# The two ends of a causal attention kernel: x ahead of the weights, filler on the identity, the last sums on TensorE, the third half inverted through DRAM

## The chip, the cores and the metric

The kernel runs on one core of one Trainium2 chip. The metric is the device time of one execution in microseconds (us). Before the change it is the median of three runs. The profile is one execution taken by the hardware profiler; its times count from the first instruction, and its span is a little shorter than the time of the run.

## The reference

One layer over x of shape (32, 256, 32, 32), all in float32. x is normalised over groups of 8 channels, projected to queries, keys and values by 1x1 convolutions, and attention with 8 heads of 32 dimensions runs over the 1024 positions of each image. A position sees only positions before it; the first one sees none. The result is added to x.

```python
q = jnp.einsum('oc,bcs->bos', q_w, xf) + q_b[None, :, None]
kv = jnp.einsum('oc,bcs->bos', kv_w, xf) + kv_b[None, :, None]
k, v = (kv[:, :EMBED_C], kv[:, EMBED_C:])
...
mask = jnp.tril(jnp.ones((S, S), dtype=x.dtype), -int(MASK_CENTER))
scores = jnp.einsum('bhqd,bhkd->bhqk', q, k) / jnp.sqrt(jnp.asarray(dk, x.dtype))
scores = jnp.where(mask == 0, jnp.asarray(-10000.0, x.dtype), scores)
attn = jax.nn.softmax(scores, axis=-1)
attn = jnp.where(mask == 0, jnp.asarray(0.0, x.dtype), attn)
out = jnp.einsum('bhqk,bhkd->bhqd', attn, v)
...
x = x + _L0_conv_ref(_gn(x), L0_conv_q_w, L0_conv_q_b, L0_conv_kv_w, L0_conv_kv_b)
```

## The kernel before

**Tiling.** Channels lie on the 128 partitions in two groups (`NG = 2`, four heads each); the 1024 positions are cut into two halves of 512 (`NH = 2`). Group and half together give four results per image, numbered n = 0 to 3, each a tile of 128 x 512. Scores are computed transposed, keys on partitions, without a shift by the maximum: `scores` (L303) makes them on TensorE, ScalarE takes exponentials into tiles `e` (four heads x 512) and `eh` (four heads x 256), GpSimd cuts the diagonal (`mask`, L285). `values` (L341) multiplies by v into `acc`, one visit later, and VectorE adds the exponentials up in the first `e` tile of each result, called `total` (L358). The denominator is the sum of `total` over the partitions, a product with a matrix of ones (`sum_keys`, L388, result `pd`).

**Order.** An image is N = 12 visits. The list `visits` says which pieces of scores a visit makes, `products` which pieces are multiplied after it. Everything else of an image hangs on a visit number: `at` holds calls made after the scores of a visit, `after` calls made after its values. The order of TensorE, ScalarE, VectorE and GpSimd is the order in which the program writes the calls (`tc.manual_schedule`). Each engine runs its queue in that order, so an instruction that waits holds back all that stand behind it. SyncE issues loads and stores, also in one order; ScalarE issues the loads of the weights and biases.

**Start.** x of images 0 and 1 is loaded on SyncE in halves by channel group (`load`, L113). ScalarE issues the three weights, the query bias, the key bias and the value bias (`load_weights`, L134). TensorE turns each weight by transposing products (`turn_weights`). VectorE takes the statistics (`norm_channels`), TensorE averages them over a group of channels (`norm_mean`, `norm_variance`), VectorE forms the variance (`norm_deviation`, tile `dev`), GpSimd the power of -1/2, VectorE the normalised x (`norm_apply`, tile `xn`). `keep_busy` (L151) makes products that nobody reads. The query bias is multiplied by the scale of the scores on VectorE at L566, behind `norm_apply`. Then the first projections (`pp`) run.

**Denominators.** For most images the totals are folded by DMA and inverted in a compact form: sums to DRAM, back as 128 rows of 64 (`gather`, tile `rows`), a check that they are in range and a reciprocal on VectorE (`check_sums`, `invert`), the inverses to DRAM, and from there broadcast to 32 partitions per head (tile `rb`). `finish` (L459) multiplies, adds the bias and x, and stores.

**End.** In the last image (b = 31) results 0 and 1 go that way, and GpSimd and ScalarE finish them (`finish_aside`). Results 2 and 3 are inverted in place: `check_here` and `invert_here` work on 128 x 512 tiles, the sum of the heads standing on all 32 partitions of each. The denominator of result 3 is put together on TensorE by `sum_pieces` (L395): first `total`, which VectorE has added up as far as visit N-2, and then the pieces of the last two visits, which aren't added on VectorE (`summed` is false in the last visit of scores and behind it). `end_last` (L492) checks and inverts result 3 in two halves of 256 columns; it also forms `outside`, the number that says whether any sum was out of range (then the whole is computed again in another way, which doesn't happen here).

```python
when(first + N, lambda b=b: check_here(2, in_range[:, ROW : ROW + 1]))
when(first + N, lambda b=b: invert_here(b, 2, slice(0, HALF)))
when(first + N, lambda b=b: finish(b, 2))
for n in every[:2]:
    when(first + N, lambda b=b, n=n: finish_aside(b, n), after)
```

Of the kernel before, what the change touches and what calls it, by code (L numbers as in the profile page):

```python
# [9 lines left out]
F32 = mybir.dt.float32  # L10
# [7 lines left out]
P = 128  # L18
HD = 32
CPG = 8  # L20
HALF = 512
# [10 lines left out]
def tile_norm_attention_residual(  # L32
# [64 lines left out]
        compare_op=ALU.is_ge, fill=0.0, base=CPG - 1, channel_multiplier=-1,  # L97
    )
    avg = avg.rearrange("p a b -> p (a b)")
    in_range = const.tile([P, ROW + 1], F32, name="in_range")  # L100
    nc.gpsimd.memset(in_range, 1.0)
    eps = const.tile([P, 1], F32, name="eps")
    nc.gpsimd.memset(eps, 1e-5)
# [5 lines left out]
    def unshifted():  # L109
# [1 line left out]
        bank_free = tc.alloc_semaphore("bank_free")  # L111
        xpool = tc.alloc_tile_pool(name="xpool", bufs=4)

        def load(b):
            live["x", b] = xpool.tile([P, NG, S], F32, tag="x", name=f"x_{b}")
            for g in range(NG):
                nc.sync.dma_start(out=live["x", b][:, g, :], in_=x_in[b, :, g, :])

        for b in range(min(2, B)):
            load(b)  # L120
        work = tc.alloc_tile_pool(name="work", bufs=2)
        qkpool = tc.alloc_tile_pool(name="qkpool", bufs=3)
        epool = tc.alloc_tile_pool(name="epool", bufs=3)
# [7 lines left out]
        def misc(name):  # L131
            return ps_m.tile([P, HALF], F32, tag="misc", name=name)
# [17 lines left out]

        def keep_busy(n):  # L151

            pt = ps_s.tile([P, 2, HALF], F32, tag="sT", name=f"busy_{n}")
            for _ in range(n):
                nc.tensor.matmul(pt[:, 0, :C], lhsT=ident, rhs=live["wn", 0][:, 0, :], start=True, stop=True)  # L155

        def spare(name):

# [233 lines left out]
                    start=start, stop=stop, skip_group_check=True,  # L392
                )

        def sum_pieces(b, pieces, start, stop):  # L395

            if start:
                live["pd", b] = misc(f"pd_{b}")
                sum_keys(live["pd", b], live["sum", b, NG - 1, NH - 1], slice(0, HALF), slice(0, HALF), True, False)
            for pc in pieces:  # L400
                e = live.pop(("e", b, pc))
                for kb, cols, of in pc[4]:
                    sum_keys(live["pd", b], e, cols, of, False, stop and pc is pieces[-1])

        def sums(b, g, hf):

            n = NH * g + hf
            total = live.pop(("sum", b, g, hf))
            if (b, n) == (B - 1, 3):
                pd = live["pd", b]  # L410
            else:
                pd = misc(f"pd_{b}_{n}")
                sum_keys(pd, total, slice(0, HALF), slice(0, HALF))
            den = small.tile([P, HALF], F32, tag="den", name=f"den_{b}_{n}")
            if b == B - 1 and n >= 2:

                most = small.tile([P, 1], F32, tag="most", name=f"most_{n}")
                nc.scalar.activation(den, pd, AF.Identity, accum_out=most)
                live["most", n], live["den", n] = most, pd if n == 3 else den
                return  # L420
            nc.scalar.copy(den, pd)
            if n == 0:
                live["sums", b] = dram.tile([4, 4, HALF], F32, tag="sums", name=f"sums_{b}")
            nc.sync.dma_start(out=live["sums", b][n], in_=den[::HD, :])
# [41 lines left out]
                nc.vector.tensor_copy(rb[:, 0:1], xt[:, g, 0:1])  # L466
            nc.sync.dma_start(out=x_out[b, :, g, cols], in_=rb)

        def check_here(n, ok):

            least = small.tile([P, 1], F32, tag="least", name=f"least_{n}")
            junk = small.tile([P, HALF], F32, tag="den", name=f"junk_{n}")
            nc.vector.tensor_scalar(junk, live["den", n], SUM_MIN, 1.0, ALU.is_ge, ALU.min, accum_out=least)
            nc.vector.scalar_tensor_tensor(ok, live["most", n], SUM_MAX, least, ALU.is_le, ALU.mult)

        def invert_here(b, n, within):
            rb = live["rb", b, n] if within.start else inverses(b, n)
            nc.vector.reciprocal(rb[:, within], live["den", n][:, within])  # L478

        def finish_aside(b, n):  # L480

            g, hf = divmod(n, NH)
            cols = slice(hf * HALF, (hf + 1) * HALF)
            num, rb, xt = live["num", b, n], live["rb", b, n], live["x", b]
            nc.gpsimd.tensor_tensor(rb, num, rb, ALU.mult)
            nc.gpsimd.tensor_tensor(rb, rb, xt[:, g, cols], ALU.add)
            nc.scalar.activation(rb, rb, AF.Identity, bias=v_bias_col[:, g : g + 1])
            if hf == 0:
                nc.scalar.copy(rb[:, 0:1], xt[:, g, 0:1])
            nc.sync.dma_start(out=x_out[b, :, g, cols], in_=rb)  # L490

        def end_last(b):  # L492


            worst = const.tile([P, 1], F32, name="worst")
            ok = const.tile([P, 1], F32, name="ok")
            nc.vector.tensor_reduce(worst, in_range, AX.X, ALU.min)
            check_here(3, ok)
            both = [slice(c * HALFBANK, (c + 1) * HALFBANK) for c in range(2)]
            invert_here(b, 3, both[0])  # L500
            pc = ps_o.tile([P, HALF], F32, tag="acc", name="pc")
            nc.tensor.matmul(pc[0:1, 0:1], lhsT=worst, rhs=ok, start=True, stop=True)
            outside = const.tile([1, 1], I32, name="outside")
            nc.vector.tensor_scalar(outside, pc[0:1, 0:1], -1.0, float(P), ALU.mult, ALU.add)
            finish(b, 3, both[0])
            invert_here(b, 3, both[1])
            finish(b, 3, both[1])
            return outside

# [39 lines left out]
        every = range(4)  # L549

        with tc.manual_schedule(engines={ENG.PE, ENG.Activation, ENG.DVE, ENG.Pool}):
            load_weights()
            turn_weights(0)
            for g in range(NG):
                norm_channels(0, g)
            keep_busy(2)
            norm_mean(0)
            turn_weights(1)
            norm_deviation(0)
            norm_variance(0)  # L560
            norm_rstd(0)
            turn_weights(2)
            keep_busy(4)
            for hf in range(NH):
                norm_apply(0, slice(hf * HALF, (hf + 1) * HALF))
            nc.vector.tensor_scalar_mul(qk_bias[:, 0, :], qk_bias[:, 0, :], SCALE)  # L566
            units = projections(0)
            for n, f in zip((None, None, 0, 0, 0, 0) + PROJECT[6:], units):
                if n is None:
# [5 lines left out]
            for b in range(B):  # L575
# [6 lines left out]
                    prepare(b, [first + n for n in PREPARE])  # L582
                for n in every:
                    v = first + (N if last and n == 3 else SUMS[n])
                    if last and n == 3:
                        for i in (N - 1, N):
                            when(first + i, lambda b=b, i=i: sum_pieces(b, products[i - 1], i == N - 1, i == N), after)
                    if late:
                        when(v, lambda b=b, n=n: sums(b, *divmod(n, NH)), after)
                    else:  # L590
                        when(v, lambda b=b, n=n: fold(b, n, 2 * HD), after)
                        when(v + 2, lambda b=b, n=n: fold(b, n, HD), after)
                        when(v + 4, lambda b=b, n=n: stack(b, n))
                if not last:
                    if not late:
                        when(first + N + 6, lambda b=b: sum_folded(b), after)
                    v = first + N + (2 if late else 8)
                    when(v, lambda b=b: gather(b, every))
                    when(v + 2, lambda b=b: check_sums(b, every))
                    when(v + 2, lambda b=b: invert(b, every))  # L600
                    for n in every:
                        when(first + FINISH[late][n], lambda b=b, n=n: finish(b, n), after)
                else:
                    when(first + N - 4, lambda b=b: gather(b, every[:2]))
                    when(first + N - 3, lambda b=b: check_sums(b, every[:2]))
                    when(first + N - 3, lambda b=b: invert(b, every[:2]))
                    when(first + N, lambda b=b: check_here(2, in_range[:, ROW : ROW + 1]))
                    when(first + N, lambda b=b: invert_here(b, 2, slice(0, HALF)))
                    when(first + N, lambda b=b: finish(b, 2))
                    for n in every[:2]:  # L610
                        when(first + N, lambda b=b, n=n: finish_aside(b, n), after)
            for i in range(B * N + 1):
                if i < B * N:

                    between = at.pop(i, ()) if i % N == 6 else ()
                    scores(i // N, *visits[i % N], between)
                for f in at.pop(i, ()):
                    f()
                if i:
                    for pc in products[(i - 1) % N]:  # L620
                        values((i - 1) // N, pc, i < B * N - 1)
                for f in after.pop(i, ()):
                    f()
            assert not at and not after
# [158 lines left out]
```

## Time and profile before

| | us |
|---|---|
| median of three runs | 1878.86 (1873.87, 1878.86, 1880.27) |
| the profiled run, and the span of its profile | 1876.05, 1874.0 |
| TensorE busy | 1850.8 |
| VectorE busy | 1573.4 |
| ScalarE busy | 1413.7 |
| GpSimd busy | 765.5 |
| first projection begins | 14.57 |
| last VectorE operation begins | 1869.20 |

Busy is the time in which an engine had an instruction under way. In the timeline each row has its start, its duration, the engine (PE is TensorE, PEld its loads of weights, DVE VectorE, ACT ScalarE, POOL GpSimd; SPq and ACTq are the issues of transfers on SyncE and ScalarE), the line of the kernel, the operation and its tiles; in square brackets stands how long the engine had been idle and what ended that. A transfer's row is its issue only; when it lands is seen from those who wait for it, and from the DMA packets of a window.

### The profile page before, as it was taken

Reading aid. Unit: us, or ns where it says so; the run is one execution under the profiler, and the core shown is the slowest. Engines: PE = TensorE matmul, PEld = TensorE weight load, DVE = VectorE, ACT = ScalarE, POOL = GpSimd, SP = SyncE. Lnnn points to the kernel's source line nnn. Section 1 sums busy time; section 2 is a strip of 40 time slices with the busy share of each in tenths; the row PEclk is TensorE's granted clock in tenths of the full one; section 3 lists DMA queues with packets and bytes.
Section 4 is the critical chain, followed back from the end, with each engine's and each line's share of the span. In section 5 each row is a group of like instructions: output and inputs, shape, how many; then the busy total and the mean of one; then the engine's idle time right before and its main releaser. Section 6 shows DMA issues by size and latency. Waiting matters only on the chain.

```text
span 1874.0 us, 54145 instructions
## 1 busy us (share of the span) xinstructions
PE 1850.8 (99%) x23410; PEld 950.6 (51%) x23410; DVE 1573.4 (84%) x1604; ACT 1413.7 (75%) x1775; POOL 765.5 (41%) x741
## 2 busy tenths in 40 slices
PE   8999999999999999999999999999999999999997
PEld 4555555555554555555555545455555555455543
DVE  3778988888988889888889888898888888888878
ACT  5777777777777777777777777777777777777775
POOL 1443443434434434434344344343343443443413
PEclk9999999999999999999999999999999999999998
DMA  3446665666666666665666656766556666666412
GB/s 119 69 79 144 138 145 118 117 137 138 140 123 127 125 140 139 145 121 111 137 138 142 145 105 123 140 138 148 117 114 140 138 143 116 133 123 140 95 50 81
DMA packets 77516, 233.41 MB, mean 125 GB/s; under 512 B 19808, under 2 KB 20832, under 8 KB 61912
## 3 DMA queue, kind: packets, MB, share of 16 engines
q0 software_dynamic: 15360, 94.39, 34.4%
q1 hardware_dynamic: 60280, 134.72, 24.7%
q8 instruction: 185, 3.03, 0.7%
q10 hardware_dynamic: 1632, 0.79, 0.1%
q14 instruction: 59, 0.48, 0.1%
HBM read 68.41 MB, written 35.62 MB: 56 GB/s over the span
## 4 chain that ended last, share of the span: by engine, by line
PE 97%; DVE 1%; DMA 0%; ACT 0%; issue 0%; ACTq 0%; DVEq 0%
PE sT L277 31%; PE acc L353 26%; PE pp L169 25%; PE ppv L169 13%; PE pd L390 2%; DVE e L358 1%; DMA wn<-in_L_conv_kv_w_dram 0%; DVE rb L464 0%; DVE rb L463 0%; DVE rb L478 0%; ACT e L331 0%; PE pv L169 0%; PE busy L155 0%; ACT k L231 0%; PE pm L169 0%
## 5 line engine op out<-in xcount | busy, mean ns | idle before, releaser
L331 ACT ACTIVATE e<-sT 128x1024 f32<-128x1024 f32 x768 | 748.3, 1022 | 365.4 <-PE sT L277 283.2
L358 DVE TENSOR_TENSOR e<-e,eh 128x1024 f32<-128x1024 f32 x382 | 534.5, 1413 | 247.2 <-PE acc L353 215.1
L292 POOL TENSOR_SCALAR_AFFINE_SELECT e<-e 128x512 f32<-128x512 f32 (+1 forms) x256 | 359.4, 1404 | 678.5 <-ACT e L331 657.9
L358 DVE TENSOR_TENSOR e<-e,e 128x1536 f32<-128x1536 f32 x381 | 618.0, 1622 | 16.9 <-POOL e L292 2.6
L277 PE MATMUL sT<-q,k 32*128 32x256 f32 (+3 forms) x7168 | 617.6, 460 | 0.8 <-ACT k L231 0.8
L277 PEld LDWEIGHTS sT<-q,k 32*128 32x128 f32 x7168 | 463.4, 184 | 163.7 <-ACT q L231 50.6
L169 PE MATMUL pp<-xn,wT 128*32 128x512 f32 x4096 | 492.2, 598 | 0.0
L353 PE MATMUL acc<-e,v 128*32 128x512 f32 (+2 forms) x4096 | 401.1, 486 | 0.0
L329 ACT ACTIVATE eh<-sT 128x1024 f32<-128x1024 f32 x384 | 395.6, 1030 | 0.0
L371 POOL DMA_DIRECT2D e<-e x240 | 199.5, 892 | 388.0 <-PE sT L277 159.5
L169 PE MATMUL ppv<-wT,xn 128*32 128x256 f32 x4096 | 247.3, 382 | 0.0
L353 PEld LDWEIGHTS acc<-e,v 128*32 128x32 f32 x4096 | 132.9, 110 | 223.6 <-issue 201.1
L353 PE MATMUL acc<-eh,v 128*32 128x256 f32 x3072 | 224.4, 379 | 0.0
L169 PEld LDWEIGHTS pp<-xn,wT 128*32 128x32 f32 x4096 | 107.0, 109 | 218.2 <-issue 199.3
L353 PEld LDWEIGHTS acc<-eh,v 128*32 128x32 f32 x3072 | 98.5, 110 | 164.2 <-issue 152.6
L169 PEld LDWEIGHTS ppv<-wT,xn 128*32 128x32 f32 x4096 | 120.2, 109 | 102.0 <-issue 32.1
L292 POOL TENSOR_SCALAR_AFFINE_SELECT eh<-eh 128x512 f32<-128x512 f32 x128 | 160.6, 1255 | 0.1
L464 DVE SCALAR_TENSOR_TENSOR rb<-rb,v_bias_col,x 128x512 f32<-128x512 f32 (+1 forms) x127 | 114.1, 898 | 4.5
L463 DVE TENSOR_TENSOR rb<-num,rb 128x512 f32<-128x512 f32 (+1 forms) x127 | 90.4, 711 | 11.6 <-DMA rb<-inverses 11.3
L231 ACT ACTIVATE k<-pp,qk_bias 128x512 f32<-128x512 f32 x128 | 89.4, 698 | 13.5 <-PE pp L169 12.4
L214 DVE TENSOR_SCALAR xn<-x,mean,rstd 128x512 f32<-128x512 f32 x128 | 96.7, 796 | 2.0 <-POOL rstd L207 2.0
L231 ACT ACTIVATE q<-pp,qk_bias 128x512 f32<-128x512 f32 x128 | 89.9, 702 | 4.0 <-PE pp L169 4.0
(69 smaller groups left out, 515.2 us busy)
## 6 DMA issues: line engine op xcount, KB each, us to landing
e<-e POOLq DMA_DIRECT2D x120, 512.0 KB, 8.0
x<-in_x_dram SPq DMA_DIRECT2D x64, 512.0 KB
out_dram<-rb SPq DMA_DIRECT2D x127, 256.0 KB
rb<-inverses SPq DMA_DIRECT2D x126, 256.0 KB
e<-e POOLq DMA_DIRECT2D x120, 256.0 KB, 5.0
folded<-e SPq DMA_DIRECT2D x120, 256.0 KB
rows<-sums SPq DMA_DIRECT2D x31, 32.0 KB
inverses<-inv SPq DMA_DIRECT2D x31, 32.0 KB
```

Of the source, the lines that this page charges most:

```text
L169: nc.tensor.matmul(out[part], lhsT=lhsT[:, part], rhs=rhs, start=start, stop=stop, skip_group_check=True)
L214: nc.vector.tensor_scalar(live["xn", b][:, g, cols], live["x", b][:, g, cols], mean[:, g : g + 1], rstd[:, g : g + 1], ALU.subtract, ALU.mult,
L231: nc.scalar.activation(live[key][:, cols], pp, AF.Identity, bias=qk_bias[:, n, g : g + 1], scale=(SCALE, 1.0)[n],)
L277: ins = nc.tensor.matmul(pair[:, cols], lhsT=live["k", b, g][rows, kb * P : (kb + 1) * P], rhs=live["q", b, g][rows, hf * HALF + of.start ...
L292: nc.gpsimd.affine_select(out=diagonal, in_=diagonal, pattern=[[0, 4], [0, n], [1, P]], compare_op=ALU.is_gt, fill=0.0, base=0, channel_mu ...
L329: exp = nc.scalar.activation(eh.rearrange("p (n bank) q -> p bank n q", n=2), short, AF.Exp)
L331: nc.scalar.activation(e[:, 2 * a : 2 * a + 2, :], pairs[a], AF.Exp)
L353: nc.tensor.matmul(acc[HD * j : HD * (j + 1), of], lhsT=live["v", b][:, kb, h * HD : (h + 1) * HD], rhs=e[:, j, cols], start=first, stop=l ...
L358: nc.vector.tensor_add(total[:, :, of], total[:, :, of], e[:, :, cols])
L371: nc.gpsimd.dma_start(out=total[:rows], in_=total[rows : 2 * rows], accum_op=ALU.add)
L463: nc.vector.tensor_mul(rb, num[:, within], rb)
L464: nc.vector.scalar_tensor_tensor(rb, rb, v_bias_col[:, g : g + 1], xt[:, g, cols], ALU.add, ALU.add)
```

## The change

At the start x of image 0 is loaded in four parts (half a channel group each) instead of two, and ScalarE first computes an exponential of a column of ones, which brings its table load ahead of the weights' loads. The filler products take the identity on both sides, 128 columns instead of 256, so that they need no weight; there are 12 at the very start and more between the steps of the norm. K and V weights are turned behind the variance product rather than one on each side of it. The scaling of the query bias moves ahead of `norm_deviation`.

At the end the third result of the last image (n = 2) is inverted through DRAM like the first two. Of the last result's exponentials one piece more (`eh` of the third last visit's pair, `products[N - 3][1]`) is left to TensorE, whose sum now begins with the pieces as they come and takes `total` in late (`sum_piece`, `sum_total`). The first half of the last result is finished on GpSimd and ScalarE.

```diff
-        def load(b):
+        def load(b, parts=1):
...
-        for b in range(min(2, B)):
-            load(b)
+        load(0, NH)
+        if B > 1:
+            load(1)
...
-                nc.tensor.matmul(pt[:, 0, :C], lhsT=ident, rhs=live["wn", 0][:, 0, :], start=True, stop=True)
+                nc.tensor.matmul(pt[:, 0, :P], lhsT=ident, rhs=ident, start=True, stop=True)
...
+            junk = small.tile([P, 1], F32, tag="most", name="junk")
+            nc.scalar.activation(junk, ones, AF.Exp)
             load_weights()
+            keep_busy(12)
             turn_weights(0)
             for g in range(NG):
                 norm_channels(0, g)
-            keep_busy(2)
+            nc.vector.tensor_scalar_mul(qk_bias[:, 0, :], qk_bias[:, 0, :], SCALE)
+            keep_busy(3)
             norm_mean(0)
-            turn_weights(1)
+            keep_busy(4)
             norm_deviation(0)
             norm_variance(0)
             norm_rstd(0)
+            turn_weights(1)
             turn_weights(2)
-            keep_busy(4)
+            keep_busy(5)
             for hf in range(NH):
                 norm_apply(0, slice(hf * HALF, (hf + 1) * HALF))
-            nc.vector.tensor_scalar_mul(qk_bias[:, 0, :], qk_bias[:, 0, :], SCALE)
...
-                    when(first + N, lambda b=b: check_here(2, in_range[:, ROW : ROW + 1]))
-                    when(first + N, lambda b=b: invert_here(b, 2, slice(0, HALF)))
+                    when(first + N - 2, lambda b=b: gather(b, every[2:3]))
+                    when(first + N - 2, lambda b=b: check_sums(b, every[2:3]))
+                    when(first + N - 2, lambda b=b: invert(b, every[2:3]))
                     when(first + N, lambda b=b: finish(b, 2))
...
-                if i:
-                    for pc in products[(i - 1) % N]:
-                        values((i - 1) // N, pc, i < B * N - 1)
+                for n, pc in enumerate(products[(i - 1) % N] if i else ()):
+
+                    summed = i < B * N - 2 or (i == B * N - 2 and n == 0)
+                    values((i - 1) // N, pc, summed)
+                    if i == B * N:
+                        sum_piece(B - 1, pc, stop=n == 1)
+                        if n == 0:
+                            sum_total(B - 1)
+                if i == B * N - 1:
+                    for n, pc in enumerate(products[N - 2] + products[N - 3][1:]):
+                        sum_piece(B - 1, pc, start=n == 0)
...
-            finish(b, 3, both[0])
-            invert_here(b, 3, both[1])
+            finish_aside(b, 3, both[0])
+            nc.vector.reciprocal(rb[:, both[1]], pd[:, both[1]])
             finish(b, 3, both[1])
```

## The prediction

> **What bounds the kernel now.** I read the page's chain first, then the timeline of the first 20 us and of the last 40 us, then DMA by windows in both. The chain:
>
> ```profile
> PE 97%; DVE 1%; DMA 0%; ACT 0%; issue 0%; ACTq 0%; DVEq 0%
> ```
>
> TensorE is the whole middle, and the diff leaves the middle alone. What can move is the 14.6 us before the first projection and the 20 us after TensorE first runs dry (1854). A delay at the start passes through whole, since TensorE bounds everything behind it. The start, from the timeline (start, duration, engine, line, operation, tiles, count, idle before and its releaser):
>
> ```profile
> 8.83 0.16 DVE L194 TENSOR_TENSOR dev<-mv,mean 128x2 f32<-128x2 f32 x1 [0.68 <-ACT mean L187]
> ...
> 11.41 1.92 DVE L214 TENSOR_SCALAR xn<-x,mean,rstd 128x512 f32<-128x512 f32 x4 [2.03 <-POOL rstd L207]
> 11.53 2.71 PEld L155 LDWEIGHTS busy<-wn,ident 128*128 128x128 f32 x8
> 11.74 2.90 PE L155 MATMUL busy<-wn,ident 128*128 128x256 f32 x8
> ...
> 14.57 3.64 PE L169 MATMUL pp<-xn,wT 128*32 128x512 f32 x32
> ```
>
> The normalised half is there at 11.41 + 0.96 = 12.4, but the q product begins at 14.57: the V weights landed at 10.8, and turning them and the filler held TensorE until then. The norm chain has 2.2 us of slack. The query bias is scaled at 13.24, behind `norm_apply`. When did it land? DMA from 8 to 9 us, then from 9 to 10:
>
> ```profile
> DMA packets 191, 0.40 MB, mean 403 GB/s; under 512 B 4, under 2 KB 122, under 8 KB 191
> ```
>
> ```profile
> DMA packets 750, 0.32 MB, mean 317 GB/s; under 512 B 644, under 2 KB 683, under 8 KB 750
> ```
>
> The biases are 4-byte packets, issued from 2.35 on. They run after 9 us only, behind the three weights in ScalarE's queue.
>
> The end, on SyncE's queue (three issues that follow each other):
>
> ```profile
> 1847.76 0.49 SPq L447 DMA_DIRECT2D inverses<-inv  x1
> 1850.87 1.19 SPq L450 DMA_DIRECT2D rb<-inverses  x2
> 1852.11 11.52 SPq L467 DMA_DIRECT2D out_dram<-rb  x2
> ```
>
> and by windows (busy of PE, PEld, DVE, ACT, POOL; clock, DMA share, GB/s):
>
> ```profile
> 1855.00:1856.00 1.00, 0.00 (x0) 0.00 (x0) 1.00 (x2) 0.00 (x0) 1.00 (x1) 1.00 0.26 68
> 1857.00:1858.00 1.00, 1.00 (x12) 0.36 (x8) 1.00 (x2) 0.00 (x0) 0.92 (x2) 0.50 0.27 100
> 1859.00:1860.00 1.00, 1.00 (x12) 0.44 (x8) 1.00 (x1) 0.00 (x0) 1.00 (x2) 0.50 0.00 0
> ```
>
> The two broadcasts `rb<-inverses` hold a quarter of the DMA (4 of 16 engines) until 1858.6, and TensorE runs at half its clock after its 2 us gap at 1854 to 1856. VectorE, which sets the end:
>
> ```profile
> 1851.69 2.28 DVE L358 TENSOR_TENSOR e<-e,e 128x2048 f32<-128x2048 f32 x1
> 1854.07 1.94 DVE L358 TENSOR_TENSOR e<-e,eh 128x1024 f32<-128x1024 f32 x1
> ...
> 1857.75 3.34 DVE L478 RECIPROCAL rb<-den 128x512 f32<-128x512 f32 x1
> ...
> 1869.20 0.48 DVE L464 SCALAR_TENSOR_TENSOR rb<-rb,v_bias_col,x 128x256 f32<-128x256 f32 x1
> ```
>
> **What the Trainium skill says.** "DMA: Bandwidth & Descriptors", section "Why a DMA increments its semaphore by 16 and not by 1": a DMA is split over the largest number of engines up to 16 that divides the slowest dimension of both sides, on SP's and ACT's queues the lowest-numbered ones. A broadcast of 4 rows, or a store of 4 rows, thus uses 4. The trace agrees: share 0.26 here, and 0.25 to 0.27 from 1827 to 1837 for the four broadcasts of image 30, some 2.6 us each. Same page, "Queues, rings and completion order": each engine takes a queue's descriptors in order. The biases above agree. "TensorE: Matmul & The Clock Gate", "Part 1: The HAM clock gate": half clock until some 3.4 us of activity; the trace shows 0.50 at 1857 and turnings at 1.12 us per weight at the start. "ScalarE: Activation LUTs", "What ACT_TABLE_LOAD costs": 1.28 us; the trace has 1.28.
>
> **The change part by part. Start.** (a) x_0 comes in four loads, so its last quarter leaves one `bn_stats` (0.65) instead of two behind it: 0.6 us off `mv`. (b) The table load and an exponential of `ones` stand before the weights' loads on ScalarE. If the issue waits for them, weights and biases start 1.5 us later (0.81 to 2.3); if ScalarE's sequencer runs ahead, only the wait for `ones` (1.05) counts, 0.3. No trace row decides it; x_0 then lands up to 0.7 earlier. (c) The scaling of `qk_bias` is moved ahead of `norm_deviation` on VectorE. This adds a wait: `dev` and all of the norm behind it now queue behind a load that itself queues behind all the weights. In the trace of before that load is used at 13.24; SyncE's wait on its slot ended by 11.2, and its packets ended not before 9.7, so it lands between 10.3 and 11.2. After: 10.8 + 0.3 to 1.5 with some relief from the x already gone; 11.0 to 12.3. I take 11.8, against 8.83 for `dev` before. From there: three small operations and the way to TensorE 0.7, the variance product 0.3, `rstd` and `pow` 1.1, the first xn 0.5 to 1.0: 14.4 to 14.9. On TensorE both turnings now stand behind the variance product (12.8): 2 x 1.12 = 15.0. Then the filler: 10 passes of 128 columns where 8 of 256 took 2.90, so 10 x 0.18 = 1.8: 16.8. (d) The early filler hides beside x's loading; it does not carry a warm clock over the 2 to 3 us wait. The q product starts at 16.8 instead of 14.57: +2.2, I take +2.0. Ends: 11.0 with a warm clock gives 14.5 (0); 12.3 and all cold gives 17.6 (+3.0).
>
> **End.** Removed from VectorE: the last add of `eh` (1.94), the check of the third half (0.67 + 0.08 + 1.17), its reciprocal (3.34): 7.2 us; first half of the last `finish` (0.9) goes to GpSimd and ScalarE beside the second reciprocal (1.75). TensorE gets 8 more passes of 256 columns (0.6), beside its old gap. Added: the third half goes den, DRAM, `rows`, check and reciprocal (0.85), DRAM, broadcast. This puts a wait for `rows` on VectorE ahead of the last full add (2.28), which TensorE's sum needs, and a wait for `rb` ahead of everything else.
>
> When does `rows` come? On SyncE the store of the third sums stands behind the two broadcasts (issued 1850.87 to 1852.06). It has 4 rows, so it shares their 4 engines and runs when they are through, 1858.0. Landed 1858.5. `rows` issue to use took 2.0 or more (issue 1843.33, packets until 1845.2): 1860.5. Check and reciprocal: 1861.35. Full add: 1863.65; VectorE idles from 1851.77 to 1860.5. TensorE has done all other pieces by 1858.4 and stands 5 us, so it is cold: the total (1.04 warm), acc and pd of the last `eh` (0.61 each) take 2 x 2.26 = 4.5: 1868.15, and ScalarE's sum 0.85: 1869.0. Meanwhile store of the inverses 1.45 (1823.79 to 1825.24): 1862.85; broadcast 1.35 to its first packet, 2.7 on 4 engines, 0.5 to be seen: 1867.4; `finish` and the minimum 1.85: 1869.25. So both ways meet at 1869.2. Then check 0.81, reciprocals 1.7 + 1.75, product 0.94: 1874.4 against 1869.68: +4.7. The stores behind it are as before. Ends: +2 if the sums go to free engines (`rows` at 1859.0), TensorE keeps its clock and the store is quick; +6.4 if the store of the inverses takes 3.1 as it did at 1847.76.
>
> Sum: +2.0 + 4.7 = +6.7. The four known times of before have a mean of 1877.3 and the three a median of 1878.86; I take 1878 as base: 1884.7.
>
> **The rivals.** R1, it does what it is for: `rows` and the broadcast come while VectorE is busy, TensorE never stops. Then pd is ready at 1858.4 + 2.26 + 0.85 = 1861.5 and VectorE ends 5.2 later at 1866.7: -3.0; with the bias early, -1 at the start: 1874. For it: 7.2 us less on the engine of the last chain. Against: 4 engines busy until 1858.6, and one queue. R2, part is hidden: start 0 and end +2 to +3 (low ends of both): 1880.5. For it: the norm's old slack of 2.2 us. R3, all high ends: +3.0 + 6.4, 1887.4.
>
> **How the numbers follow.** Forecast 0.50, R1 0.12, R2 0.26, R3 0.12. 0.3% is 5.6 us. Of the forecast's cases about three in four lie beyond it, and all of R3: slower 0.5 x 0.75 + 0.12 = 0.50. Of R1 some 4 in 10 reach -5.6 with noise: faster 0.05. The rest, 0.45, is within. The range leaves out most of R1 and the extreme of R3: 1877 to 1889.5; it takes in the bounds 0 to +3.0 and +2 to +6.4 on base 1877 to 1879.
>
> **What would show it.** Start: `dev` waits behind the scaling of `qk_bias`, at 11 to 12.3, released by a load of the bias, and pp starts at 15.5 to 17. Wrong if `dev` is before 9.5. End: VectorE idle for some 8 us before the `in_range` operation on 32 rows, TensorE idle after 1858, clock 0.5 behind it, and a second wait of VectorE for rb<-inverses. If the sums' store passes the broadcasts, `rows` comes before 1856 and R1 holds. If the middle changes its length, nothing of this explains it.

## The result, and the profile after

Six runs of the changed kernel took 1885.1 us (median, 1881.47 to 1886.69), six of the kernel before 1879.57 (1873.87 to 1882.17). The ratio is 1.0033 with a 95% interval of 1.0013 to 1.0053, or +6.2 us (2.4 to 10); the two medians by themselves lie 5.5 us apart. The profiled execution had a span of 1883.2 us against 1874.0.

The two profiles are 9.2 us apart, and two instants that both kernels have split this in three. The first q product begins at 15.12 instead of 14.57: +0.55 at the start. The check of the sums of results 0 and 1 (VectorE, `in_range`, 64 rows; "the 64-row check" from here on) comes at 1851.26 instead of 1846.81, so the middle took 3.9 us more. From there to the end of VectorE's last operation it is 27.64 us instead of 22.87: +4.8 at the end.

The chain of the page of the changed kernel:

```profile
PE 95%; DMA 2%; ACT 1%; issue 1%; DVE 0%; POOL 0%; SPq 0%; POOLq 0%
```

Before, DMA had 0% of it. The 2% are three things: the load of x at the start (6.7 us), two transfers in a row that fold sums in the middle (15.6, counted whole, though TensorE waits for a part of them only) and the DRAM trips at the end (14.5). The end first, from the timeline of the changed kernel (start, duration, engine, line, operation; in brackets the idle time before it and its releaser):

```profile
1854.58 1.20 SPq L451 DMA_DIRECT2D rb<-inverses  x2
1855.84 0.51 SPq L425 DMA_DIRECT2D sums<-den  x1
...
1862.63 0.34 SPq L435 DMA_DIRECT2D rows<-sums  x1
...
1864.42 0.83 DVE L440 SCALAR_TENSOR_TENSOR in_range<-rows,in_range 32x64 f32<-32x64 f32 x1 [8.20 <-DMA rows<-sums]
...
1866.00 0.31 SPq L448 DMA_DIRECT2D inverses<-inv  x1
1866.00 2.29 DVE L361 TENSOR_TENSOR e<-e,e 128x2048 f32<-128x2048 f32 x1
1867.36 0.53 SPq L451 DMA_DIRECT2D rb<-inverses  x1
1868.35 1.93 PE L393 MATMUL pd<-e,pick 128*32 128x512 f32 x8 [6.43 <-DVE e L361]
...
1871.98 0.69 DVE L464 TENSOR_TENSOR rb<-num,rb 128x512 f32<-128x512 f32 x1 [3.68 <-DMA rb<-inverses]
...
1878.41 0.49 DVE L465 SCALAR_TENSOR_TENSOR rb<-rb,v_bias_col,x 128x256 f32<-128x256 f32 x1
```

Read it downwards: two broadcasts, then the store of the third sums, issued at 1855.84; the gather can be issued only at 1862.63, when that store has landed, 6.8 us after its issue. The store of the third inverses (1866.00) takes 1.4 us until the next issue. VectorE idles 8.20 us for the gathered rows, TensorE 6.43 us for the add that stands behind their check, and VectorE once more for the broadcast. TensorE's clock has gone down over its gap (windows; busy of PE, PEld, DVE, ACT, POOL, then the granted clock, 0.50):

```profile
1868.00:1869.00 1.00, 0.65 (x4) 0.20 (x8) 0.29 (x1) 0.00 (x0) 0.00 (x0) 0.50 0.09 31
```

The start, from the same timeline:

```profile
8.92 0.69 DVE L182 BATCH_NORM_STATS2 st<-x 128x6 f32<-128x512 f32 x1 [0.38 <-DMA x<-in_x_dram]
...
10.18 2.05 PE L158 MATMUL busy<-ident 128*128 128x128 f32 x8
...
10.67 0.17 DVE L552 TENSOR_SCALAR qk_bias<-qk_bias 128x2 f32<-128x2 f32 x1 [0.82 <-DMA qk_bias<-in_L_conv_q_b_dram]
...
12.38 1.69 PE L151 MATMUL wt<-ident,wn 128*128 128x128 f32 x8
...
15.12 1.47 PE L172 MATMUL pp<-xn,wT 128*32 128x512 f32 x9
```

The last statistics of x begin at 8.92; before, the last two began at 6.62:

```profile
6.62 1.29 DVE L179 BATCH_NORM_STATS2 st<-x 128x6 f32<-128x512 f32 x2 [0.61 <-DMA x<-in_x_dram]
```

The scaling of the bias waits 0.82 us for its load with `dev` right behind it, and the 8 filler passes take 2.05 us.

### The profile page after: what moved, and what is told of

It is laid out like the page before. It is cut to its first block, busy times and chain, and to the rows that moved or that the text cites. A ratio compares the mean times of both kernels' runs of the same rounds, so it can differ in the third digit from the quotient of the medians.

```text
span 1883.2 us, 54242 instructions
## 1 busy us (share of the span) xinstructions
PE 1855.5 (99%) x23454; PEld 955.4 (51%) x23454; DVE 1564.5 (83%) x1600; ACT 1414.5 (75%) x1776; POOL 765.5 (41%) x743
## 4 chain that ended last, share of the span: by engine, by line
PE 95%; DMA 2%; ACT 1%; issue 1%; DVE 0%; POOL 0%; SPq 0%; POOLq 0%
PE sT L280 31%; PE acc L356 25%; PE pp L172 25%; PE ppv L172 12%; PE pd L393 2%; DMA folded<-e 1%; ACT e L334 0%; DMA sums<-den 0%; DMA x<-in_x_dram 0%; ACT k L234 0%; DMA e<-e 0%; DMA rb<-inverses 0%; PE pv L172 0%; PE busy L158 0%; PE pm L172 0%
## 5 line engine op out<-in xcount | busy, mean ns | idle before, releaser
L465 DVE SCALAR_TENSOR_TENSOR rb<-rb,v_bias_col,x 128x512 f32<-128x512 f32 x126 | 110.7, 879 | 4.5
L464 DVE TENSOR_TENSOR rb<-num,rb 128x512 f32<-128x512 f32 x126 | 89.1, 708 | 28.1 <-DMA rb<-inverses 23.7
L234 ACT ACTIVATE k<-pp,qk_bias 128x512 f32<-128x512 f32 x128 | 89.4, 698 | 13.5 <-PE pp L172 12.4
```

The lines of the kernel that those rows point to most:

```text
L234: nc.scalar.activation(live[key][:, cols], pp, AF.Identity, bias=qk_bias[:, n, g : g + 1], scale=(SCALE, 1.0)[n],)
L464: nc.vector.tensor_mul(rb, num[:, within], rb)
L465: nc.vector.scalar_tensor_tensor(rb, rb, v_bias_col[:, g : g + 1], xt[:, g, cols], ALU.add, ALU.add)
```

## The experiments

Twelve kernels were run. The table gives what their traces show (us). "q" is the first q product, "middle" from there to the 64-row check. The next three columns count from that check: when the gathered third sums are used, when `rb_2` is used, when the last store has been issued. "folded" adds up TensorE's waits ahead of the products of the rows folded by DMA, from 30 to 1840. Each row is one profiled execution, and some of these were not typical: that of end_only was the fastest of its 9 runs, that of both_best the slowest of 14, that of end_pool the second slowest of 22.

| kernel | q | middle | sums | rb_2 | last store | folded |
|---|---|---|---|---|---|---|
| before | 14.57 | 1832.2 | - | - | 23.2 | 1.7 |
| after | 15.12 | 1836.1 | 13.2 | 20.7 | 28.3 | 4.3 |
| start_only | 13.53 | 1835.4 | - | - | 23.0 | 3.6 |
| end_only | 15.37 | 1830.6 | 12.8 | 21.1 | 28.7 | 0.3 |
| sums_first | 13.51 | 1833.2 | 13.1 | 20.8 | 28.6 | 2.6 |
| sums_aside | 13.15 | 1834.7 | 12.0 | 20.0 | 27.6 | 3.8 |
| sums_ahead | 15.20 | 1837.7 | 7.5 | 18.0 | 25.5 | 5.8 |
| before_slack | 14.81 | 1835.1 | - | - | 23.0 | 0.2 |
| start_slack | 13.97 | 1835.3 | - | - | 23.0 | 0 |
| end_best | 14.08 | 1835.5 | 5.1 | 12.8 | 23.8 | 3.9 |
| both_best | 13.96 | 1837.8 | 5.2 | 12.9 | 24.3 | 4.7 |
| no_early_filler | 16.03 | 1835.4 | - | - | 23.0 | 4.4 |
| end_pool | 13.18 | 1841.0 | 5.2 | 16.2 | 23.9 | 7.4 |
| end_pool_old | 14.92 | 1833.0 | 6.3 | 17.1 | 24.4 | 2.2 |

**One end alone.** start_only is the kernel before with the start of the diff, end_only the changed kernel with the start of before. The edit of each is whole hunks of the diff, for end_only:

```diff
-load(0, NH)
-if B > 1:
-    load(1)
+for b in range(min(2, B)):
+    load(b)
...
-nc.scalar.activation(junk, ones, AF.Exp)
 load_weights()
-keep_busy(12)
 turn_weights(0)
...
```

> The change's start with the end of before. Theory A (the change costs some 0.5 us at the start and 4.8 us at the end; the rest of the difference between the two profiles, 3.9 us in the middle, is DMA chance that comes and goes with the execution): first q product at 15.1 us (before 14.57), VectorE from the 64-row range check to its last operation as in before (22.8 us), time +0.5 us, ratio 1.000 to 1.001. Theory B (the start's new order of loads costs the middle its 3.9 us): waits of TensorE for the folded sums add up to 3 us or more again, and the ratio is 1.002 to 1.003.

> The change's end with the start of before. Theory A: first q product at 14.57 us, VectorE from the 64-row range check to its last operation 27.6 us against 22.8 before, ratio about 1.0025. Theory B (the end costs less than the two profiles suggest, since the rest was the start or the middle): ratio within 1.001.

start_only: 1878.76 us (22 runs) against 1877.84 (32 runs of before), ratio 1.001 (0.9999 to 1.002). end_only: 1881.37 us, ratio 1.0028 (1.0017 to 1.0038), which is +5.3 us (3.2 to 7.1); its last store is issued 28.7 us behind the 64-row check against 23.2. So the end costs what the trace says, some 5 us, alone. At the start theory A had the wrong sign: the q product is at 13.53, a microsecond earlier than before. Theory B has the waits that it expected, 3.6 us with a middle of 1835.4, but not its ratio of 1.002 to 1.003: part of the loss is hidden by the earlier start.

Why 13.53 here and 15.12 in the changed kernel, with the same code? The timeline of start_only:

```profile
9.78 1.16 PE L158 MATMUL busy<-ident 128*128 128x128 f32 x8
...
10.43 0.17 DVE L563 TENSOR_SCALAR qk_bias<-qk_bias 128x2 f32<-128x2 f32 x1 [0.97 <-DMA qk_bias<-in_L_conv_q_b_dram]
...
11.39 1.09 PE L151 MATMUL wt<-ident,wn 128*128 128x128 f32 x8
...
13.53 2.78 PE L172 MATMUL pp<-xn,wT 128*32 128x512 f32 x24
```

The filler takes 1.16 us instead of 2.05, two turnings 1.09 instead of 1.69: here TensorE kept its full clock over the wait for x, and the profiled execution of the changed kernel had lost it. Of the eight profiles with this start and its early filler, six show 1.16 and two (after, sums_ahead) 1.94 to 2.05.

**Without the early filler.**

```diff
 load_weights()
-keep_busy(12)
 turn_weights(0)
```

> The change's start on the end of before, without its 24 early filler passes. If they keep TensorE's clock up until the norm's products (against predicted step d): four turnings of the query weights take 1.1 us (0.60 to 0.72 with the filler), the 8 passes ahead of the variance product 1.7 us or more (1.16), the turnings of key and value weights 1.7 to 2.2 (1.10), and the q product begins 1.3 to 2 us later than in start_only, at 14.8 to 15.5 us. If they do nothing for the clock behind the wait for x, these times and 13.5 us stay.

```profile
5.19 1.09 PE L151 MATMUL wt<-ident,wn 128*128 128x128 f32 x4 [5.19 <-DMA wn<-in_L_conv_q_w_dram]
...
9.86 2.08 PE L158 MATMUL busy<-ident 128*128 128x128 f32 x8
...
12.09 1.97 PE L151 MATMUL wt<-ident,wn 128*128 128x128 f32 x8
```

In this timeline the turnings and the filler ahead of the q product all run at about half speed, and the q product begins at 16.03, later than the 14.8 to 15.5 expected and 2.5 us later than in start_only (one execution, 1881.53 us). In this one profile the new start without its early filler is slower than the old one, whose q product begins at 14.57 to 15.37.

**The queue at the end.** sums_first takes the broadcasts out of `invert` (as `spread`) and asks for them behind the gather, but SyncE's queue isn't among the engines whose order is written out, and its order came out as in the changed kernel.

```diff
 when(first + N - 2, lambda b=b: gather(b, every[2:3]))
+when(first + N - 2, lambda b=b: spread(b, every[:2]))
```

> The changed kernel, with the store and the gather of the third sums put ahead of the two broadcasts on SyncE's queue. Theory A (the store of 4 rows was late because it stood behind the broadcasts on their 4 engines): the gathered sums are used within 6 us of the 64-row range check instead of 13.2 us, VectorE idles under 2 us ahead of the 32-row check, TensorE's gap ahead of the full total falls from 6.4 us to under 3, and VectorE's end comes 5 to 7 us earlier, at 21 to 22.5 us behind the 64-row check. Theory C (a store of the sums and its gather through DRAM take some 8 us by themselves): the gathered sums still come 12 us or more behind the 64-row check, and the end stays within 1 us of the changed kernel's.

So it says nothing on theory A or C; it is the changed kernel once more: ratio 1.0034 (1.0021 to 1.0046), sums used at 13.1 us. In sums_aside the store alone goes to another queue:

```diff
-nc.sync.dma_start(out=live["sums", b][n], in_=den[::HD, :])
+queue = nc.scalar if (b, n) == (B - 1, 2) else nc.sync
+queue.dma_start(out=live["sums", b][n], in_=den[::HD, :])
```

> The changed kernel, with the store of the third sums alone issued from ScalarE's queue instead of SyncE's; the broadcasts stay where they are. If order within one queue holds the store up (A1), it now lands within 3 us of its issue (it took 6.78). If it is the 4 engines that the broadcasts occupy, whatever the queue (A2), it lands some 4 to 5 us after its issue or later, when the broadcasts are half or wholly through. If neither (C), 6.8 us again.

```profile
1849.12 1.06 ACTq L426 DMA_DIRECT2D sums<-den  x1
1851.15 1.20 SPq L452 DMA_DIRECT2D rb<-inverses  x2
...
1852.91 0.47 SPq L436 DMA_DIRECT2D rows<-sums  x1
...
1859.78 0.22 DVE L441 SCALAR_TENSOR_TENSOR in_range<-rows,in_range 32x64 f32<-32x64 f32 x1 [7.43 <-DMA rows<-sums]
```

The store is issued so early that it never meets the broadcasts: the trace has its four packets, the only ones of 2 KB in ScalarE's queue then, at 1850.34 to 1850.53, and the broadcasts are issued at 1851.15. So the run says nothing on A1 or A2. But now the gather is issued behind the broadcasts, and it takes 6.9 us (1852.91 to 1859.78), where in the changed kernel, with the broadcasts through, it took 1.8 (1862.63 to 1864.42). Its packets show how: 24 of the 32 run from 1854.8 to 1855.3, the other 8, a quarter, only at 1858.8 to 1859.3, when the broadcasts end. The delay goes to the small transfer that comes behind the broadcasts. sums_ahead puts both ahead, with an explicit issue order:

```diff
+def spread_behind(b, ns):
+    with tc.issue_after(live["gathered"].ins):
+        spread(b, ns)
```

> The changed kernel, with SyncE's queue now held to the order: store of the third sums, their gather, and only then the two broadcasts. Theory A (store and gather were late because they stood in one queue behind the broadcasts on their 4 engines): the gathered sums are used some 7.5 to 9 us behind the 64-row range check (13.2 in the changed kernel), TensorE's gap ahead of the full total falls from 6.4 to under 2 us, VectorE ends 21 to 23.5 us behind the 64-row check (27.6), and the time falls by about 5 us against the changed kernel, ratio to before 1.000 to 1.001. Theory C (a store of 4 rows of sums and its gather take that long by themselves): 12 us or more, VectorE's end within 1 us of the changed kernel's, ratio 1.003 again.

```profile
1860.38 0.75 DVE L440 SCALAR_TENSOR_TENSOR in_range<-rows,in_range 32x64 f32<-32x64 f32 x1 [2.49 <-DMA rows<-sums]
...
1862.25 0.32 SPq L448 DMA_DIRECT2D inverses<-inv  x1
...
1864.60 1.07 PE L393 MATMUL pd<-e,pick 128*32 128x512 f32 x8 [1.02 <-DVE e L361]
...
1866.31 0.52 SPq L455 DMA_DIRECT2D rb<-inverses  x1
...
1870.94 0.69 DVE L472 TENSOR_TENSOR rb<-num,rb 128x512 f32<-128x512 f32 x1 [6.39 <-DMA rb<-inverses]
```

Theory A holds for the sums: used 7.5 us behind the check instead of 13.2, and TensorE's gap falls to 1.02 us. Theory C is out. Another rival, that the store of image 30's result (256 KB), issued between the third sums and their gather, holds them up, is out too: it stands ahead of the gather here as well. But the broadcasts now stand ahead of the third inverses: their store takes 4.1 us (1862.25 to 1866.31) where the changed kernel needed 1.4 (1866.00 to 1867.36), and VectorE's wait only moved, from the first DRAM trip to the second. VectorE ends 24.9 us behind the check where 21 to 23.5 was expected, and the last store comes 2.8 us earlier. The time, ratio 1.004 (1.0026 to 1.0053), doesn't show even this: TensorE waited 5.8 us for folded rows in the middle of the profiled execution. One more execution, of 9303.7 us, is not in the ratio; nothing here explains it.

end_best puts the broadcasts of results 0 and 1 behind that of result 2, and the third gather ahead of the last store of image 30 (`behind` is `issue_after` once more):

```diff
-when(first + N - 2, lambda b=b: gather(b, every[2:3]))
+when(first + N - 3, lambda b=b: gather(b, every[2:3]), after)
+when(first + N - 3, lambda b=b: behind("gathered", finish, b - 1, 3), after)
...
 when(first + N - 2, lambda b=b: invert(b, every[2:3]))
+when(first + N - 2, lambda b=b: behind("spread", spread, b, every[:2]))
```

> The changed kernel with SyncE's queue put in the order in which results are needed: store and gather of the third sums ahead of the last store of image 30, then the third inverses and their broadcast, and the broadcasts of results 0 and 1 last. Theory A (what cost the change its 4.8 us at the end is the queue alone): the third sums are used 5 to 6.5 us behind the 64-row range check (13.2), rb_2 is used by 12.5 us (20.7), TensorE shows no gap over 1 us ahead of the full total and keeps its clock, VectorE ends 18 to 20 us behind the 64-row check, against 27.6 in the changed kernel and 22.8 in before; ratio to before 0.997 to 0.999, with the middle's chance in it. Theory D (reciprocal and sums on TensorE bound the end as they did before, and the DRAM way brings nothing even when it is hidden): 22.5 us or more, ratio 1.000 or above.

```profile
1854.66 0.22 DVE L440 SCALAR_TENSOR_TENSOR in_range<-rows,in_range 32x64 f32<-32x64 f32 x1
...
1855.62 0.33 SPq L448 DMA_DIRECT2D inverses<-inv  x1
...
1856.99 1.77 SPq L455 DMA_DIRECT2D rb<-inverses  x3
...
1862.36 0.69 DVE L472 TENSOR_TENSOR rb<-num,rb 128x512 f32<-128x512 f32 x1 [4.45 <-DMA rb<-inverses]
...
1864.95 1.26 POOL L483 TENSOR_TENSOR rb<-num,rb 128x512 f32<-128x512 f32 x1 [5.45 <-DMA rb<-inverses]
...
1872.83 0.54 SPq L476 DMA_DIRECT2D out_dram<-rb  x1
```

Sums at 5.1 us and `rb_2` at 12.8: VectorE's wait for the sums is gone, its wait for `rb_2` (4.45 us) ends 7.9 us sooner than in the changed kernel, and TensorE's clock stays at 1.00. VectorE ends 20.9 us behind the check, 6.7 earlier than in the changed kernel. But now GpSimd, which does results 0 and 1, gets `rb_0` at 15.4 us instead of 8.7 (1860.00 in the changed kernel), and is the last: the last store is issued at 23.8, near where the kernel before has it (23.2). The step that was not priced: three broadcasts of 4 rows on the same engines come one behind the other, and somebody waits for the third. That also explains VectorE's 20.9 where 18 to 20 was expected: its last two operations (1868.33 and 1869.12) now run beside GpSimd's late ones and take 0.75 and 1.37 us, against 0.42 and 0.49 in the changed kernel. The gain in time that theory A expected (0.997 to 0.999) isn't there: ratio 1.0018 (1.0007 to 1.0028).

end_pool issues these two from GpSimd's queue, in its idle time:

```diff
+queue = nc.gpsimd if b == B - 1 and ns.start == 0 else nc.sync
-nc.sync.dma_start(
+queue.dma_start(
```

> As end_best (the changed kernel, its start included), but the broadcasts of results 0 and 1 are issued from GpSimd's queue in a stretch in which GpSimd idles, so that they stand neither ahead of the third sums nor behind the third inverses. Theory A (with the queue out of the way the DRAM way is hidden): the third sums used by 6 us behind the 64-row check, rb_2 by 12.8 us, GpSimd begins on results 0 and 1 by 11 us (15.4 in end_best), and the last store is issued 20 to 21.5 us behind the 64-row check, against 23.8 in end_best, 28.3 in the changed kernel and 23.2 in before. Time 2 to 3 us below end_best. Rival (4 engines are shared by any queue): rb_2 or the inverses' store comes 2 us or more later than in end_best and the last store is at 23 us or later.

```profile
1858.55 1.48 POOL L456 DMA_DIRECT2D rb<-inverses  x2
...
1860.38 0.32 SPq L448 DMA_DIRECT2D inverses<-inv  x1
...
1865.33 0.58 SPq L456 DMA_DIRECT2D rb<-inverses  x1
...
1870.35 0.69 DVE L473 TENSOR_TENSOR rb<-num,rb 128x512 f32<-128x512 f32 x1 [7.67 <-DMA rb<-inverses]
```

The times are the rival's: the inverses' store takes 4.95 us with the broadcasts in another queue, and the last store is at 23.9 us. But the store is not alone in its queue. Ahead of it, issued at 1859.16, stands image 30's last store (256 KB), whose 128 packets of 2 KB run from 1860.1 to 1863.8; in sums_ahead, with no broadcast under way, they ran within 0.9 us. From 1861.75 to 1863.3 SyncE's queue moved 24 of them and 4 small packets, GpSimd's queue 51 packets of the broadcasts. So it is not the order within a queue alone: broadcasts in GpSimd's queue slow down what SyncE's queue carries. How long a small store alone beside them takes was not run. Time 1879.9 us, ratio 1.0005 (0.9995 to 1.0015).

**The middle.** The kernels with `slack` take the sum over the folded rows one visit later:

```diff
-when(first + N + 6, lambda b=b: sum_folded(b), after)
+when(first + N + 7, lambda b=b: sum_folded(b), after)
```

> The kernel before, with the sum over the folded rows taken one visit (about 3.7 us) later, so that TensorE meets it with more time for the folding transfers. Theory M (the differences in the middle are TensorE's waits for folded rows, which come by chance of the transfers): these waits vanish from the trace, TensorE's gaps between first projection and the end fall from 3.65 us to 2 or less, the middle (first to last exponential) takes 1830 to 1831 us in place of 1832.5, and the time falls by 2 to 4 us with less scatter. Theory N (they are something else that moves with TensorE): the gaps move to another instruction, time within 1 us of before.

> The change's start on the kernel before, with the same later sum over folded rows. Theory M: with the waits gone the start's own effect is left: first q product at 13.2 to 13.6 us when TensorE's clock stays up, 15.1 when not, against 14.6 to 15.4; time 1 us below that of before_slack. Theory B (the new order of loads makes the middle longer): middle 2 us or more longer than in before_slack, time equal to it or above.

The waits are gone, and with them much of the scatter: 21 runs of before_slack lie between 1877.73 and 1881.28 us, 22 of start_slack between 1876.99 and 1880.19, where before itself, on the same chip, goes from 1873.14 to 1884.92. So the scatter comes with these waits. But it is no faster: the middle is 1835 us in both, some 3 us above that of before, so the later place costs TensorE more than the waits did. What the traces show of it: ScalarE's copies behind these products (`den`) now wait for TensorE 30 times, 35.6 us in sum, against 3 times and 2.5 us in before. Whether that is the cost was not tested. The ratios (1.0008 and 1.0007) don't part the two kernels, as the scatter of before is in both. Put side by side, their medians, 1879.95 and 1878.11, give the start 1.8 us of gain with the middle quiet; in the two profiles the q product is 0.84 earlier (13.97, where 13.2 to 13.6 was expected). Without the later place the same start gained nothing (start_only: 1.9 us lost, -0.2 to 3.8). This pair of differences is the best sign in the run times that the start's gain is lost in these waits.

**Whether the start makes the middle wait.** end_pool_old is end_pool with the start of before.

> The same end with the start of before. Theory G (the change's start gains some 1.5 us by the first q product and the middle then waits 2 to 3 us more for folded rows): first q product 1 to 2 us later than in end_pool, TensorE's waits for folded rows in the middle under 2 us (2.7 to 5.8 with the change's start), time equal to end_pool's or up to 2 us below. Theory H (these waits are chance, whatever the start): as many waits as in end_pool within the scatter, and the time 1 to 2 us above end_pool's.

Waits for folded rows, by engine and releaser, longest in the last column. In end_pool:

```profile
PE pd L393 <- ACT num L364: 3.5, 2, 1.8
PE pd L393 <- DMA folded<-e: 2.0, 2, 1.7
PE pd L393 <- issue: 1.9, 1, 1.9
```

In end_pool_old:

```profile
PE pd L390 <- ACT num L361: 0.9, 1, 0.9
PE pd L390 <- ACT e L331: 0.7, 1, 0.7
PE pd L390 <- DMA folded<-e: 0.6, 1, 0.6
```

These products read `folded`, which a DMA writes; where the releaser named is ScalarE, it can have been done before: of the two such waits in end_pool the one that ends at 630.55 stands behind a copy that was through at 629.61. 7.4 against 2.2 us, and 1878.08 us (14 runs) against 1879.9 (22), ratio 0.9999 (0.9986 to 1.0013), though end_pool begins its q product 1.74 us earlier. Theory G has the trace on its side, here and in the table: without slack, nine profiles with the changed start or a variant of it show 2.6 to 7.4 us of such waits, three with the start of before 0.3 to 2.2, with no overlap; but each is a single execution, and end_pool's and end_only's, at the two ends, are among the untypical ones. The times only lean the same way, for the intervals overlap. What in the first 15 us does this to transfers hundreds of microseconds later was not found. both_best, with as many x loads as before, has 4.7 us of waits, but in its slowest execution, so the number of loads isn't ruled out.

**Both ends mended.** both_best is end_best with x_0 in two loads, the bias scaled behind `norm_apply`, and less filler.

```diff
-load(0, NH)
+load(0)
...
+turn_weights(1)
-keep_busy(4)
 norm_deviation(0)
```

> As end_best, and at the start x_0 in two loads, the scaling of the query bias back behind the norm's application, the first turning of the key weights back ahead of the variance product, and the filler behind the turnings cut from 10 to 4 passes; table load and early filler stay first. If the quarter loads and the wait for the bias held the norm (predicted steps a and c): mv is there by 8.2 us (9.3 to 9.7 in the profiles of the change's start), dev by 8.8 (10.1 to 10.8), the first q product begins at 12 to 12.8 us (13.2 to 15.1). If x comes late because it shares the DMA with the weights whatever the cut, mv stays behind 9 us and the q product at 13 or later. Time 1 us below end_best in the first case.

It took 1877.74 us (14 runs), ratio 0.999 (0.998 to 1.0), where the changed kernel has 1.0033: level with before, with nothing won. `mv` is begun at 8.04 and `dev` at 8.89, as expected, but the q product only at 13.96, since TensorE first waits for the value weights and turns them; both_best and then before:

```profile
12.05 1.12 PE L151 MATMUL wt<-ident,wn 128*128 128x128 f32 x4 [1.60 <-DMA wn<-in_L_conv_kv_w_dram]
```

```profile
10.83 1.12 PE L148 MATMUL wt<-ident,wn 128*128 128x128 f32 x4 [0.81 <-DMA wn<-in_L_conv_kv_w_dram]
```

In the packets of the traces x_0's 1 MB is through at about 5.7 us here and 7.2 to 7.7 with four loads (start_only, after), the last weight packet at 11.4 here and 8.8 to 9.6 there: between these starts what x gains the weights lose. It is not the whole of it, for before has x as early (5.8) and its weights at 9.9.

## Why the prediction was right, and where it was not

The time holds (1884.7 predicted, 1885.1 measured), and so does the difference (+6.7 predicted, +6.2 measured, 2.4 to 10). Of its two terms one is right; the other is wrong, and a loss in the middle that the prediction put at nothing made up for it. That is luck.

**The end, +4.7: right, step by step.** Shifting the changed kernel's times by the 4.45 us by which its 64-row check is later, they compare directly. `rows` used: 1860.5 predicted, 1859.97 measured. Full add done: 1863.65 and 1863.84. TensorE's last sums done, at half clock: 1868.15 and 1867.54. `rb_2` used: 1867.4 and 1867.53. VectorE's end: 1874.4 and 1874.45. The cause given, a store of 4 rows behind two broadcasts on their 4 engines, is shown by sums_ahead and sums_aside: move the small transfers ahead and the delay leaves them, move one and it falls on the next, with a quarter of the gather's packets waiting for the broadcasts to end. "DMA: Bandwidth & Descriptors" in the Trainium skill, section "Queues, rings and completion order", says that an engine takes turns between queues packet by packet. The packets of end_pool agree, 28 of SyncE's queue among 51 of GpSimd's, and show its limit: the small store, with a larger one ahead of it in its own queue, still took 4.95 us against 1.4.

**The start, +2.0: wrong, sign included.** Over the eight profiles with the diff's start and its early filler the q product begins at 13.15 to 15.20, mean 13.97; over four with the start of before at 14.57 to 15.37, mean 14.92: 1 us gained. None reached the 15.5 to 17 that the prediction gave as its sign.
- Steps (a) and (b), `mv` 0.6 earlier and x_0 up to 0.7 earlier: the reverse. The last quarter is there at 8.22 to 9.00 instead of the second half at 6.62.
- Step (b), the weights' loads: the lower end. The first weights' load is issued at 1.09, while ScalarE's table load runs from 0.81 to 2.09.
- Step (c): the wait for the bias is there, but `dev` comes at 10.13 to 11.17, not 11.8, and most of the delay is x's: ScalarE copies `mean` at 9.61 to 10.38 (8.64 before), and `dev` follows 0.4 to 1.1 us behind it where it was 0.19, so the bias adds 0.2 to 0.9. Turnings and filler, priced cold at 2.24 and 1.8, took 1.09 to 1.10 us in six of the eight profiles (1.69 and 1.81 in the other two) and 1.28 in all eight.
- Step (d), that the early filler doesn't carry a warm clock over the wait: this is the step that failed most. no_early_filler gives what (c) and (d) priced, 16.03 against the 16.8 computed; with the filler it is 13.5 in start_only. "TensorE: Matmul & The Clock Gate" in the same skill ("Part 1: The HAM clock gate"), cited for the warm-up, says too that its window of 3.4 us runs freely and isn't started by the kernel. That two profiles in eight lost their clock and six kept it agrees with that, but the waits that lost it, 1.80 and 1.81 us, are shorter than such a window and than some that kept it (1.06 to 2.07), so what decides stays open.

**The middle, 0: wrong.** "The diff leaves the middle alone" is true of its instructions. The time still went up there: start_only loses 1.9 us (-0.2 to 3.8) although its q product is 1 us earlier, with the middle quiet the same start gains 1.8, and the waits for folded rows are 2.6 to 7.4 us with this start. The prediction said that a change in the middle's length would be explained by nothing in it, and so it is. The sum came out right because a wrong +2.0 at the start stood for a gain of 1 there and a loss of about 2 to 4 in the middle. That these waits exist and that the scatter goes with them is shown; that the start raises them is what twelve profiles and the slack pair suggest, with no mechanism.

## What to carry to other kernels

A broadcast of few rows is cheap in bytes and dear in time. Here one of 4 rows and 256 KB held a quarter of the DMA for some 2.6 us, and a store of 8 KB, a gather of 8 KB or another broadcast behind it waited for it. Before sending data through DRAM, list what is queued ahead on those engines. Reordering helped only until the next consumer waited for the broadcast that was put last. When a change touches the two ends only, split the measured time at instants that both kernels have, over more than one profile, and compare each profile's time with the runs of its kernel; the middle can move without one changed instruction.

## What the runs showed of the hardware that had not been expected

- TensorE's clock outlived idle stretches of 1.06 to 2.07 us after 24 early filler passes in six profiles of eight, and was lost over 1.80 and 1.81 us in two.
- With each half of x_0 cut into two loads its last part was used later, not earlier: 8.22 to 9.00 against 6.62, and 6.72 in both_best, which goes back to two loads. Microsecond by microsecond from 4 to 7, the DMA moved 245, 325 and 289 GB/s in the changed kernel and 378, 358 and 350 in start_only, against 417, 374 and 403 in before.
- ScalarE's sequencer issues DMAs (at 1.09) while a table load (0.81 to 2.09) is in progress.
- A store of 8 KB took 1.4 us with nothing ahead of it, 4.1 us behind two broadcasts of 256 KB, and 4.95 us with the broadcasts in another queue and a store of 256 KB ahead of it in its own.
- Two VectorE operations took 0.75 and 1.37 us beside GpSimd's (end_best), and 0.42 and 0.49 in the changed kernel.
